# Square root of the fractional mix: GpSimd power in the copies, in place of ScalarE's activation

## The chip, the cores and the metric

One core of one Trainium2 chip runs the kernel. The metric is device time in microseconds (us) of one execution. Before the change it is 3354.84 us, the median of 2 runs (3348.12 and 3361.56 us). The engines are named as in the profile: PE is TensorE's matmuls, PEld its weight loads, DVE is VectorE, ACT is ScalarE, POOL is GpSimd, and SP is the queue that issues DMAs.

## What is computed

A batch of 32 images of 96 channels and 56x56 pixels goes through two residual layers, each behind a group normalisation. The first is a quantised expansion, depthwise convolution and projection. The second works on three groups of 32 channels: a gated 3x3 convolution, a fractional Fourier transform with a mix of its real and imaginary parts, and a Fourier mix; a 3x3 convolution over all 96 channels follows. The change is in the magnitude of the middle group.

```python
x = x + _L0_conv_ref(_gn(x), ...)
x = x + _L1_conv_ref(_gn(x), ...)

# inside layer 1
x_0, x_05, x_1 = (x[:, :C0], x[:, C0:C - C0], x[:, C - C0:])
...
Fre = _frft2d(x_05, _frft_mat(H, alpha), _frft_mat(W, alpha))
Mix = jnp.concatenate([Fre.real, Fre.imag], axis=1)
Mix = _group_conv(Mix, conv05_w[None] * Y[..., None, None], conv05_b, 0)
Fre_out = jax.lax.complex(Mix[:, :C1], Mix[:, C1:])
IFRFT = jnp.abs(_frft2d(Fre_out, _frft_mat(H, -alpha), _frft_mat(W, -alpha))) / (H * W)
...
out = jnp.concatenate([x_0, IFRFT, x_1], axis=1)
out = jax.lax.conv_general_dilated(out, conv2_w, (1, 1), [(1, 1), (1, 1)], ...)
```

## The kernel before

The kernel works image by image, with channels on partitions. Three streams of steps are laid into one another: the head of layer 0 (statistics, normalisation and the split of the input into a high and a low part), its body (expansion on TensorE, quantisation on ScalarE, depthwise convolution, projection) and layer 1 of the image before.

Two planners set the order. `arrange` merges the three streams step by step, by the work that each step declares for each engine. Then the class `Order` takes the instructions so recorded, works out who needs whom (`needs`), gives each a duration, a lag and, for DMAs, a transfer time (`model`), and lays them out engine by engine in simulated time (`pack`, called by `schedule`). `hold` writes the order down as it was found, so that each engine and each DMA queue takes its instructions in that order, one after the other. All durations in it are fixed formulas; for POOL it is 0.1 us and 2.25 ns per column with two wide inputs, 1.1 ns with one, and 0.5 us for up to 8 columns. Two VectorE or GpSimd instructions that `model` marks with `port` are not laid side by side.

The steps around the change, for each image:

- `split` (L704 to L710): VectorE normalises a quarter of the image into `v`, ScalarE rounds it to `hi` (L707), POOL subtracts to `lo` (L708), and POOL scales the image once, at the last quarter (L710). `hi` and `lo` feed the expansion on TensorE (L717), whose results ScalarE quantises (L662) and VectorE shifts as 32-bit words (L666).
- `group_stats` (L641 to L655): mean and variance; the reciprocal root is a power with exponent -0.5 on POOL over one column of 96 partitions (L654), once for each layer.
- `gate_row` and `gates`: a sigmoid (L911, L923) and a sine (L964) on ScalarE, each with a load of its table.
- `mix_f(h)` for the halves h = 0 and 1 of the image's rows: two times four matmuls (L1047) give the real and the imaginary part of four strips of 7 rows, on 4 x 32 partitions and 392 columns. ScalarE squares both into `sq` (L1054), VectorE adds them (L1055), ScalarE takes the square root in place (L1056), with a table load in front where another table was there, and POOL copies each strip to its rows of the padded image `cat` (L1060), partitions 32 to 63. `sq` is a tile of the pool `p1` with tag "Z" and one buffer, so the second half's squares need the first half's copies to be done.
- `mix_t` and `spatial` write the other two groups of `cat` from ScalarE and VectorE (L1118, L1120, L1140).
- `winograd(half, part)`: VectorE transforms `cat` (L1158, L1164, L1167); its tile `U` has the tag "Z" too. `final` is the last convolution on TensorE (L1179), and VectorE adds its results to the image (L1209 to L1220).

Of the kernel before, what the change touches and what calls it, by code (L numbers as in the profile page):

```python
# [78 lines left out]
BN_EPS = 1e-5  # L79
WINDOW, CHANGE = 3.4133, 0.09  # L80
TURNS, NEAR = 8, (2.0, 4.0, 8.0)
SLACK = 0.3


# [58 lines left out]
class Order:  # L143
# [64 lines left out]
    def model(self):  # L208


        self.took, self.lag, self.port, self.move, self.kind, self.work = [], [], [], [], [], []
        for i, e, access in zip(self.ins, self.eng, self.access):
            outs, ins = [a for a, w in access if w], [a for a, w in access if not w]
            n = max([_count(a) for a, _ in access], default=1)
            psum = [self.tiles.get(a.tensor.name, "")[:2] == "ps" for a in ins]
            wide = [a for a in ins if _count(a) > 1]
            lag = {"PE": 0.2, "Pool": 0.08}.get(e, 0.04)
            port, move, kind, work = False, 0.0, None, 0.0
            if i.opcode == "DMACopy":
                took = 0.47 if e == "SP" else 0.4  # L220
                for a in (outs[0], ins[0]):
                    run = size = _bytes(a.dtype)
                    dims, n = list(a.ap), 1.0
                    if self.tiles.get(a.tensor.name, "dram") != "dram":
                        n = dims.pop(0)[1]
                        move = max(move, _count(a) * size / 7000.0 * min(n / 16.0, 1.0))
                    for _, c in dims:
                        n *= c
                    for step, c in reversed(dims):
                        if step * size == run or c == 1:  # L230
                            run *= c
                        else:
                            break
                    run = min(run, n * size / 16)
                    move = max(move, math.ceil(n * size / run / 16) * (0.011 + run / 21e3))
                lag = 1.6 + move + (0.3 if ins[0].tensor.name.startswith(("in_x", "sd", "gd")) else 0.0)
            elif e == "PE":
                cols, weights, rows = _count(ins[0]), _count(ins[1]), ins[0].ap[0][1]
                full = all(str(a.dtype) == "dt.float32" for a in ins)
                beside = weights in (G, 64) and cols >= HN  # L240
                if i.is_transpose:
                    took = max(cols / 1175.0, 0.055)
                    work = cols / 1200.0
                elif full:
                    took = 2 * max(cols / 1175.0, min(weights * 0.85e-3, 1.0), 0.05)
                    work = cols / 600.0
                else:
                    took = max(cols / (2180.0 if "float32r" in str(ins[1].dtype) else 2350.0), 0.05)
                    work = cols / 2400.0
                if beside and not i.is_transpose:  # L250
                    took, work = took * weights / 128.0, work * weights / 128.0
                kind = (0 if rows <= 32 else 1 if rows <= 64 else 2), weights if beside else 0
                work *= rows / 128.0
            elif e == "Activation":
                out = _count(outs[0])
                bias = sum(_count(a) == 1 for a in ins) > 1
                took = 0.1 + bias * 0.1 + out / 960.0 + (0.08 if out > 700 and psum[0] else 0.13 if out < 8 else 0.0)
            elif e == "DVE":
                port = n > 8 and not any(psum)
                if port and i.opcode == "TensorScalarPtr" and len(wide) == 1:  # L260
                    took = 0.15 + n / 1920.0 + (0.12 if n >= 700 else 0.0)
                else:
                    port = port and len(wide) > 1
                    took = (0.14 if n > 8 else 0.16) + n / 960.0 + (0.06 if any(psum) and "ScalarPtr" in i.opcode else 0.0)
            elif e == "Pool":
                port = True
                took = 0.1 + n * (2.25 if len(wide) > 1 else 1.1) / 1000.0 if n > 8 else 0.5
            else:
                took = 0.1
            self.took.append(took)  # L270
            self.lag.append(lag)
            self.port.append(port)
            self.move.append(move)
            self.kind.append(kind)
            self.work.append(work)

    def pack(self, before, rank, near=0.0, back=False):

        n = len(self.ins)
        then, lacks, ready = [[] for _ in range(n)], [len(p) for p in before], [0.0] * n
        for k, p in enumerate(before):
            for q in p:
                then[q].append(k)
        engines = sorted(set(self.eng))
        free, held = dict.fromkeys(engines, 0.0), dict.fromkeys(("DVE", "Pool"), 0.0)
        soon, now = {e: [] for e in engines}, {e: [] for e in engines}
        start, end, kind, moved = [0.0] * n, [0.0] * n, None, 0.0
        window, much, fast = 0, 0.0, False  # L290
        for k in range(n):
            if not lacks[k]:
                heapq.heappush(soon[self.eng[k]], (0.0, k))
        for _ in range(n):
            t, e = min((free[e] if now[e] else max(free[e], soon[e][0][0]), e) for e in engines if now[e] or soon[e])
            while soon[e] and soon[e][0][0] <= t:
                k = heapq.heappop(soon[e])[1]
                heapq.heappush(now[e], (rank[k], k))
            k = now[e][0][1]
            if e == "PE" and near and self.kind[k] != kind:  # L300
                k = min([x for x in now[e] if self.kind[x[1]] == kind and x[0] < rank[k] + near], default=now[e][0])[1]
            if k == now[e][0][1]:
                heapq.heappop(now[e])
            else:
                now[e].remove((rank[k], k))
                heapq.heapify(now[e])
            if self.port[k]:
                t = max(t, held["Pool" if e == "DVE" else "DVE"])
            took = self.took[k]
            start[k], end[k] = t, t + took  # L310
            if e == "PE" and not back:
                took += CHANGE if kind != self.kind[k] else 0.0
                kind = self.kind[k]
                x, left = t, took
                while left > 1e-9:
                    while x >= (window + 1) * WINDOW - 1e-9:
                        window, fast, much = window + 1, much > 0.365 * WINDOW, 0.0
                    pace = 1.0 if fast else 0.5
                    part = min(left, ((window + 1) * WINDOW - x) * pace)
                    much += self.work[k] * part / took  # L320
                    left, x = left - part, x + part / pace
                end[k] = x
            free[e] = end[k]
            if self.port[k]:
                held[e] = end[k]
            lag = self.lag[k]
            if self.move[k] and not back:
                moved = max(moved, end[k] + 0.63) + self.move[k]
                lag = moved + self.lag[k] - self.move[k] - 0.63 - end[k]
            for q in then[k]:  # L330
                first = q if back else k
                alike = self.eng[q] == e and self.ins[first].opcode != "DMACopy"
                ready[q] = max(ready[q], end[k] + (0.0 if alike else self.lag[q] if back else lag))
                lacks[q] -= 1
                if not lacks[q]:
                    heapq.heappush(soon[self.eng[q]], (ready[q], q))
        return start, end
# [110 lines left out]
def block_kernel(ctx: ExitStack, tc: tile.TileContext, out: bass.AP, a: dict):  # L448
# [154 lines left out]

    mhalf = cp.tile([C, 1], F32, tag="mhalf", name="mhalf")
    nc.vector.memset(mhalf, -0.5)


    hids = []
# [245 lines left out]
    def layer1(i):  # L854
# [186 lines left out]
        def mix_f(h):  # L1041
# [11 lines left out]
                    )  # L1053
                nc.scalar.activation(sq[:, q, :], ps[:, :HN], AF.Square)  # L1054
            nc.vector.tensor_tensor(sq[:, 0, :], sq[:, 0, :], sq[:, 1, :], ALU.add)  # L1055
            nc.scalar.activation(sq[:, 0, :], sq[:, 0, :], AF.Sqrt)  # L1056
            for j in range(4):
                r = 1 + 14 * j + 7 * h
                src = sq[G * j : G * (j + 1), 0, :].rearrange("p (h w) -> p h w", w=W)
                nc.gpsimd.tensor_copy(cat[G : 2 * G, r : r + 7, 1 : 1 + W], src)  # L1060

        def transpose(g):

# [456 lines left out]
```

## Time and profile before

| What | Value |
|---|---|
| Median of 2 runs | 3354.84 us |
| Profiled execution, as a run | 3364.8 us |
| Profiled execution, span | 3363.0 us |
| Mean granted TensorE clock | 0.949 of full speed |
| ScalarE's square roots (L1056), 64 | 33.9 us busy |
| Table loads at L1056, 32 of 1283 ns | 41.1 us |
| Table loads at L911 and L964, 32 each | 41.1 us each |
| Copies to `cat` (L1060), 256 | 157.8 us busy, 616 ns mean |
| Subtractions `lo` (L708), 128 | 243.4 us |
| Image scaling (L710), 32 | 95.0 us |
| Powers with one column (L654), 64 | 36.0 us |

The span is the time from the first to the last instruction of one execution on the chip, and the rest of its run lies around it. Busy times are sums over one engine's instructions; engines work side by side, so they don't add up to the span. Idle time before an instruction is put down to the one that released it last. Matmul ends are modelled, and spans on POOL are rough.

### The profile page before, as it was taken

What the parts mean: (1) busy time and instruction counts of PE and PEld (TensorE: products, weight loads), DVE (VectorE), ACT (ScalarE), POOL (GpSimd) and SP (SyncE); (2) the same over time, 40 slices, a digit from 0 to 9 for tenths busy, and PEclk for the clock granted to TensorE, in tenths of its full rate; (3) what the DMA queues carried; (4) which work ended last, traced back from release to release, by engine and by line L of the source; (5) the groups of instructions that cost most, each with busy time, mean ns of one, the idle gap of its engine ahead of it and who ended that gap; (6) DMA issues with size and microseconds to landing.
All of it is one profiled execution on the core that took longest, in us unless ns stands there. A gap on an engine that the chain in (4) does not pass through costs nothing. (4 is left out here: it accounts for less than half of the span.)

```text
span 3363.0 us, 47042 instructions
## 1 busy us (share of the span) xinstructions
PE 2961.3 (88%) x17024; PEld 1824.1 (54%) x17024; DVE 2331.5 (69%) x4497; ACT 2085.9 (62%) x2792; POOL 585.2 (17%) x657
## 2 busy tenths in 40 slices
PE   3789998889998889999899999898998898999987
PEld 2455565455565555555455565455565455565544
DVE  5357677677777676777677777676777676777755
ACT  3566665576666566656566666566666576666543
POOL 3122101222101222111222011222111222101100
PEclk9898999999999999999999999999999999999987
DMA  4545564455655455654455655455655455655432
GB/s 125 150 118 143 147 166 133 116 144 144 167 159 141 117 145 137 168 141 134 124 146 151 173 146 149 121 146 138 168 157 142 116 145 143 166 162 148 115 89 51
DMA packets 436800, 469.92 MB, mean 140 GB/s; under 512 B 203174, under 2 KB 351640, under 8 KB 435544
## 3 DMA queue, kind: packets, MB, share of 16 engines
q1 hardware_dynamic: 432384, 464.18, 51.6%
q10 hardware_dynamic: 4184, 2.74, 0.3%
q8 instruction: 135, 2.21, 0.3%
q14 instruction: 97, 0.79, 0.1%
HBM read 266.85 MB, written 199.97 MB: 139 GB/s over the span
## 5 line engine op out<-in xcount | busy, mean ns | idle before, releaser
L662 ACT ACTIVATE q2s<-pd,o,s 128x784 uint8<-128x784 f32 x576 | 558.3, 1002 | 473.9 <-PE pd L756 454.5
L1179 PE MATMUL pc<-V,wcw 96*96 96x392 f32 x2304 | 834.9, 502 | 18.1 <-DVE V L1164 18.1
L662 ACT ACTIVATE q1s<-pe,o,s 128x784 uint8<-128x784 f32 (+1 forms) x640 | 624.1, 1004 | 219.7 <-PE pe L717 213.5
L717 PE MATMUL pe<-hi,w1r 96*128 96x392 f32 x1280 | 532.7, 416 | 68.0 <-ACT q1s L662 32.1
L1179 PEld LDWEIGHTS pc<-V,wcw 96*96 96x96 f32 x2304 | 366.9, 164 | 338.9 <-issue 319.7
L756 PE MATMUL pd<-d,dw 128*64 128x392 fp8e4 x4608 | 471.1, 345 | 85.1 <-DMA d<-sd 78.2
L717 PE MATMUL pe<-lo,w1r 96*128 96x392 f32 x1280 | 440.6, 344 | 3.2 <-POOL lo L708 3.2
L756 PEld LDWEIGHTS <-dw 128*64 128x64 bf16 x4608 | 243.3, 113 | 297.8 <-DMA d<-sd 104.8
L717 PEld LDWEIGHTS pe<-hi,w1r 96*128 96x128 f32 x1280 | 242.9, 190 | 181.4 <-ACT q1s L662 88.2
L708 POOL TENSOR_TENSOR lo<-v,hi 96x784 fp32r<-96x784 f32 x128 | 243.4, 1901 | 287.9 <-ACT hi L707 274.6
L1047 PE MATMUL pz<-F,g 98*32 98x392 f32 x1024 | 178.0, 700 | 129.3 <-DMA F<-pd 79.3
L786 PE MATMUL pp<-q,w3q 128*96 128x392 fp8e4 x1280 | 269.5, 359 | 12.1 <-DMA q<-gd 9.5
L717 PEld LDWEIGHTS pe<-lo,w1r 96*128 96x128 f32 x1280 | 244.2, 191 | 27.5 <-POOL lo L708 4.2
L786 PEld LDWEIGHTS <-w3q 128*96 128x96 fp8e4 x1280 | 167.2, 135 | 154.4 <-issue 70.6
L666 DVE TENSOR_SCALAR q2s<-q2s 128x392 uint32<-128x392 uint32 x288 | 119.4, 421 | 182.9 <-ACT q2s L662 180.0
L796 DVE SCALAR_TENSOR_TENSOR x<-pp,s,x 96x392 f32<-96x392 f32 x256 | 146.1, 617 | 103.9 <-PE pp L786 103.7
L654 POOL TENSOR_TENSOR stb<-veb,mhalf 96x1 f32<-96x1 f32 x32 | 17.9, 561 | 1143.8 <-DVE veb L653 1143.8
L1060 POOL COPY cat<-sq 32x392 f32<-32x392 f32 x256 | 157.8, 616 | 295.7 <-ACT sq L1056 286.1
L666 DVE TENSOR_SCALAR q1s<-q1s 128x436 uint32<-128x436 uint32 (+1 forms) x320 | 122.6, 389 | 120.5 <-ACT q1s L662 99.6
L704 DVE TENSOR_SCALAR v<-x,sta 96x784 f32<-96x784 f32 x128 | 87.0, 680 | 161.1 <-POOL lo L708 139.5
L1126 PE MATMUL ps<-s,g 128*128 128x392 f32 x512 | 193.6, 503 | 0.0
L1140 ACT ACTIVATE cat<-ps,b 32x392 f32<-32x392 f32 x256 | 158.8, 620 | 46.2 <-PE ps L1126 42.5
(156 smaller groups left out, 4267.8 us busy)
## 6 DMA issues: line engine op xcount, KB each, us to landing
d<-sd SPq DMA_DIRECT2D x288, 435.5 KB
gd<-q2s SPq DMA_DIRECT2D x288, 196.0 KB
sd<-q1s SPq DMA_DIRECT2D x256, 218.0 KB
q<-gd SPq DMA_DIRECT2D x128, 392.0 KB
x<-in_x_dram SPq DMA_DIRECT2D x128, 294.0 KB
out_dram<-x SPq DMA_DIRECT2D x128, 294.0 KB
pd<-pq SPq DMA_DIRECT2D x32, 808.5 KB
F<-pd SPq DMA_DIRECT2D x64, 392.0 KB
```

What stands on the lines that cost most here:

```text
L662: nc.scalar.activation(dst, ps, AF.Relu, bias=offset, scale=scale)
L666: nc.vector.tensor_scalar(w, w, 4, 0x0F0F0F0F, ALU.logical_shift_right, ALU.bitwise_and)
L708: nc.gpsimd.tensor_tensor(s["lo"][:, u, :], v, s["hi"][:, u, :].bitcast(F32), ALU.subtract)
L717: nc.tensor.matmul(ps[:, half, :HN], w1[:, 128 * b : 128 * (b + 1)], part[:, u, HN * half : HN * (half + 1)], start=(n == 0), stop=(n == 1),)
L756: nc.tensor.matmul(ps[64 * t : 64 * (t + 1), half, :HN], dw[n][:, 2 * t + y, :], view(s["d"][b, g][:, t, :], PQ * (14 * half + y), [[PQ, 1 ...
L786: nc.tensor.matmul(ps[:C, half, :HN], w3[:, b * C : (b + 1) * C], q2[b][:, u, HN * half : HN * (half + 1)], start=(b == 0), stop=(b == NB ...
L796: nc.vector.scalar_tensor_tensor(part, src, A3, part, ALU.mult, ALU.add)
L1047: nc.tensor.matmul(ps[G * j : G * (j + 1), :HN], s["g1"][: 3 * G + 2, G * q : G * (q + 1)], s["F"][:, 2 * HN * j + HN * h : 2 * HN * j + H ...
L1060: nc.gpsimd.tensor_copy(cat[G : 2 * G, r : r + 7, 1 : 1 + W], src)
L1126: nc.tensor.matmul(ps[:, :HN], s["g0"][:, 128 * t : 128 * (t + 1)], view(s0, PQ * (14 * half + t // 2) + t % 2, [[PQ, 14], [1, HH]]), star ...
L1140: nc.scalar.activation(dst, src, AF.Identity, bias=b0[2 * G : C], scale=1.0)
L1179: nc.tensor.matmul(ps[:C, :HN], wc[:, k, C * dx : C * (dx + 1)], V[:, :, dx : dx + W], start=(dx == 0), stop=(dx == 2),)
```

## The change

The square root on ScalarE is dropped. The four copies of each half become element-wise two-input instructions on GpSimd that raise the sum of squares to a power, with a constant 0.5 as the second input, and write it to the same rows of `cat`. The second input is a column of 128 partitions that is read with steps of zero over 7 x 56 elements. The planner that sets the order of all engines is changed as well: each DMA's lag is 0.2 us longer (`MARGIN`), and the time up to which the transfers have moved is kept for each issuing engine instead of one for all. The lines of `mix_f` stand 3 further down in the changed kernel.

```diff
+MARGIN = 0.2
 SLACK = 0.3
...
-                lag = 1.6 + move + (0.3 if ins[0].tensor.name.startswith(("in_x", "sd", "gd")) else 0.0)
+                lag = 1.6 + MARGIN + move + (0.3 if ins[0].tensor.name.startswith(("in_x", "sd", "gd")) else 0.0)
...
-        start, end, kind, moved = [0.0] * n, [0.0] * n, None, 0.0
+        start, end, kind, moved = [0.0] * n, [0.0] * n, None, {}
...
             if self.move[k] and not back:
-                moved = max(moved, end[k] + 0.63) + self.move[k]
-                lag = moved + self.lag[k] - self.move[k] - 0.63 - end[k]
+                moved[e] = max(moved.get(e, 0.0), end[k] + 0.63) + self.move[k]
+                lag = moved[e] + self.lag[k] - self.move[k] - 0.63 - end[k]
...
     mhalf = cp.tile([C, 1], F32, tag="mhalf", name="mhalf")
     nc.vector.memset(mhalf, -0.5)
+    half = cp.tile([128, 1], F32, tag="half", name="half")
+    nc.vector.memset(half, 0.5)
...
             nc.vector.tensor_tensor(sq[:, 0, :], sq[:, 0, :], sq[:, 1, :], ALU.add)
-            nc.scalar.activation(sq[:, 0, :], sq[:, 0, :], AF.Sqrt)
             for j in range(4):
                 r = 1 + 14 * j + 7 * h
                 src = sq[G * j : G * (j + 1), 0, :].rearrange("p (h w) -> p h w", w=W)
-                nc.gpsimd.tensor_copy(cat[G : 2 * G, r : r + 7, 1 : 1 + W], src)
+                power = view(half, 0, [[0, 7], [0, W]])[G * j : G * (j + 1)]
+                nc.gpsimd.tensor_tensor(cat[G : 2 * G, r : r + 7, 1 : 1 + W], src, power, ALU.pow)
```

## Prediction

> **What bounds the kernel now.** I read the page's engine shares first, then the line views of the instructions that the change touches, then the timeline around one of them. The sum below is made against the profiled execution: span 3363.0 us, 3364.8 us as a run, which lies 0.3% above the median of 3354.84 us.
>
> ```profile
> PE 2961.3 (88%) x17024; PEld 1824.1 (54%) x17024; DVE 2331.5 (69%) x4497; ACT 2085.9 (62%) x2792; POOL 585.2 (17%) x657
> ```
>
> TensorE is the engine with the least idle time: some 400 us in 32 images, and a period of about 105 us per image (3363 / 32). GpSimd (POOL) is idle 83% of the time. Nothing in this line says that POOL matters; whether it will depends only on what one power costs there. So the next view is that of single lines: minimum, median and maximum of one instruction in ns.
>
> ```profile
> L1056 ACT ACTIVATE sq<-sq x64: 517/531/545, 221.5 to 3325.3; 128x392 f32<-128x392 f32 x64
> L1056 ACT ACT_TABLE_LOAD  x32: 1283/1283/1283, 220.2 to 3319.7; - x32
> ...
> L1060 POOL COPY cat<-sq x256: 502/510/2198, 222.2 to 3329.3; 32x392 f32<-32x392 f32 x128
> ...
>   ACT sq L1054: 72.5, 24
>   DVE U L1158: 23.2, 31
> ...
> L992 POOL TENSOR_TENSOR cs<-ee,tab x64: 282/298/363, 172.6 to 3295.4; 114x57 f32<-114x57 f32 x64
> ...
> L708 POOL TENSOR_TENSOR lo<-v,hi x128: 1831/1846/2202, 42.6 to 3139.2; 96x784 fp32r<-96x784 f32 x128
> ...
> L654 POOL TENSOR_TENSOR stb<-veb,mhalf x32: 546/547/740, 134.4 to 3275.1; 96x1 f32<-96x1 f32 x32
> ```
>
> The first two lines are what goes: a square root of 531 ns on ScalarE, 64 times, and a table load of 1283 ns ahead of every second one. The third is what is replaced: eight copies of 392 columns per image, four for each half. The two lines under it are the waits on these copies: ScalarE's squares of the second half (72.5 us in 24 waits) and VectorE's first Winograd step (23.2 us in 31). The last three are all two-input POOL instructions; L654 is the one that matters, since it is already a power, with one column.
>
> ```profile
> 412.41 2.96 POOL L710 TENSOR_SCALAR x<-x,ab 96x3136 f32<-96x3136 f32 x1 [0.85 <-DVE v L704]
> ...
> 413.61 2.17 DVE L1055 TENSOR_TENSOR sq<-sq 128x392 f32<-128x392 f32 x1 [1.30 <-ACT sq L1054]
> 415.34 2.20 POOL L708 TENSOR_TENSOR lo<-v,hi 96x784 fp32r<-96x784 f32 x1
> ...
> 417.60 2.16 POOL L1060 COPY cat<-sq 32x392 f32<-32x392 f32 x4
> ...
> 419.79 0.50 ACT L1054 ACTIVATE sq<-pz 128x392 f32<-128x392 f32 x1 [3.44 <-POOL cat L1060]
> ```
>
> Start, length, engine. VectorE's add L1055 takes 568 ns at its median. Here it starts 1.20 us into POOL's L710 and lasts until 0.41 us after L710's end at 415.37: it was held for the rest of the other engine's instruction. So a POOL instruction that reads SBUF holds up a VectorE instruction with two SBUF inputs until it is over. The last line shows the other tie: ScalarE stands for 3.44 us, until the four copies have read `sq`, because the tile has one buffer (tag "Z").
>
> **The change part by part.**
>
> *Removed from ScalarE:* 64 x 0.531 + 32 x 1.283 = 34 + 41 = 75 us. The tables for the sigmoid and the sine are still loaded once per image each (the build of the changed kernel has 64 loads in the loop, against 96), so nothing is loaded in place of the third. These 75 us stand in the chain add, root, copies, Winograd; as a gain they are worth at most 75 us and at least nothing, as ScalarE is busy only 62%. I count them in full where the chain is what is waited for.
>
> *The copies become powers.* 256 instructions of 392 columns, in the same places of POOL's queue or interleaved with the `lo` subtractions. Their price d is in no row, so I bound it. From L992 and L708 a two-input instruction costs (1846 - 298) / (784 - 57) = 2.13 ns per column and 298 - 57 x 2.13 = 177 ns to start. The power L654 with one column takes 549 ns (547 and 551 in its two groups), so 549 - 177 - 2 = 370 ns belong to the power itself. One end: all of the 370 ns is set-up, paid once per instruction, and columns then stream as in a subtraction: d = 177 + 370 + 392 x 2.13 = 1.38 us. The other end: the 370 ns is the work on one column and repeats with each: d = 177 + 392 x 372 = 146 us. The ends lie a factor of 100 apart. The nearest row is the power itself, not the subtraction, so I take a price of L654's kind: a routine that is gone through per column, of which some is entry. No row splits the 370 ns; I take half and half: d = 177 + 185 + 392 x 187 = 73.7 us. Let f be the share that repeats; f = 0.5 here.
>
> [...]
>
> *Sum.* The powers take 256 x 73.7 = 18,867 us in the place of 158 us of copies. What hides that? POOL takes its queue in order: behind the first four powers stand, in most images, the other four, then the `rstd` power L654 of the next layer 1, and in many images `lo` subtractions that the next image's expansion needs. ScalarE's second squares wait for the first four powers (the wait above, 3.44 us for four copies of 0.51 us and what delayed them), and behind them in ScalarE's order stand the quantisations L662 that free TensorE's PSUM pairs. VectorE is held by the port, and its Winograd steps wait for the last four. So nearly nothing runs beside a power: VectorE gets one held instruction through between one power and the next. Of its instructions per image some 65 have inputs in SBUF alone (L666 19, L1158 8, L1217 6, L704, L885, L1164 and L1213 4 each, and smaller ones); 8 gaps let 8 of 65 pass, an eighth of the 105 us period, 13 us per image, 420 us in all. 3,365 + 18,867 - 158 - 75 - 420 = 21,580, so **21,600 us**.
>
> *The order by hand.* The planner is also changed: 0.2 us more for each DMA, and DMAs of different queues no longer behind one another in its model. It prices the power as any two-input instruction (0.1 + 392 x 2.25 / 1000 = 0.98 us), so it leaves no room for more. The order of every engine shifts. TensorE's waits on DMAs that could grow or go are 78 + 105 us (`d`) and 79 us (`F`): between -262 and +262 us; I take zero, as neither sign is favoured. The `half` constant is one 128x1 memset on VectorE ahead of the loops, under 0.2 us by its 1-column rows.
>
> **The rivals.** In all of them a chance is given beside the time.
>
> *The power streams (faster).* d = 1.38 us. POOL gains 256 x 1.38 - 158 = 195 us and stays under 25%; ScalarE loses 75 us. The chain of one half changes from 1.28 / 2 + 0.53 + 4 x 0.544 (the spacing of the copies) = 3.35 us to 5.5 us; TensorE has the next image's expansion to run meanwhile, and of its waits only 18 us fall on the Winograd transform, so the longer chain is covered and the shorter ScalarE shows: 3,365 - 75 = 3,290 us. If no part of 64 x (5.52 - 2.18) = 214 us is covered it is 3,365 + 214 - 75 = 3,504 us. For it: plain POOL instructions stream, and a first call can carry set-up. Against it: a copy of one column takes 183 ns (L1094, 64x1) and a subtraction starts with 177 ns, the power takes three times that, and every time, not the first time alone. It decides where L1060's successor records below about 2 us. Chance 0.16.
>
> *The power repeats, but the rest of the kernel runs beside it.* The port or the waits leave room and POOL alone is the bound: 18,867 + 585 - 158 = 19,294 us, plus 222 us ahead of the first copy and 33 us behind the last: 19,550 us. For it: some VectorE rows are not held (four L796 with a PSUM input run at 0.56 us each beside L708). Against it: ScalarE's wait and POOL's own order. Chance 0.17.
>
> *The power repeats and is exposed,* my forecast: 0.67. Inside these two, f is open: f = 1 gives 3,365 + 37,376 - 158 - 75 = 40,500 us with nothing hidden; f = 0.05 gives d = 177 + 352 + 392 x 20.6 = 8.6 us and 3,365 + 2,204 - 158 - 75 - 420 = 4,900 us. POOL alone is longer than the old run once 256 d + 427 > 3,365, from d = 11.5 us or f = 0.07.
>
> That the change does not do what it says is ruled out by the build: 256 two-input instructions with `half` stand on POOL, no square root is left in the loop.
>
> **How the numbers follow.** Repeating cases hold 0.84; with f even between 0 and 1, 0.95 of that lies above f = 0.05, so 4,900 to 40,500 us holds 0.80. Streaming, 0.16, splits into 0.10 faster by over 2% (the 3,290 us), 0.03 within 2% and 0.03 slower (part of the 214 us exposed). 2% is about what a measurement of this kernel can tell from no change. So faster 0.10, same 0.03, slower 0.84 + 0.03 = 0.87.
>
> **What would show it.** The power's own line with its median decides most: 73.7 us at f = 0.5, over 10 us for any slow case, 1.4 us for the rival. POOL busy should be near 89% of the span (19,294 of 21,600), TensorE's share fall to about 14%. `DVE sq`, `T` and `U` should wait for `cat` in hundreds of microseconds per image, ScalarE's squares for 4 d per image. If POOL is above 97%, the second rival holds. VectorE instructions that last as long as a power show the held port; if none does, that step is wrong though the sum may stand. A power line below 2 us makes the whole forecast wrong.

## The result and the profile after

The changed kernel takes 19,285.67 us (median of 2 runs, 19,280.35 and 19,291.0), 5.75 times the time before (95% interval 5.73 to 5.77). The page of its profiled execution opens with the busy time of each engine; the second fence below has answers by line: first minimum, median and maximum in ns of one instruction, then who waited for it, in us in all and number of waits.

```profile
span 19278.6 us, 46882 instructions
...
PE 3143.8 (16%) x17024; PEld 1962.7 (10%) x17024; DVE 2365.0 (12%) x4498; ACT 2011.6 (10%) x2696; POOL 16575.8 (86%) x657
...
L1063 POOL TENSOR_TENSOR cat<-sq,half 32x392 f32<-32x392 f32 x256 | 16141.9, 63054 | 136.6 <-DVE sq L1058 123.0
```

```profile
L1063 POOL TENSOR_TENSOR cat<-sq,half x256: 62827/62832/64502, 201.6 to 19182.3; 32x392 f32<-32x392 f32 x128
...
  ACT sq L1057: 7802.5, 32
  DVE U L1161: 3979.4, 32
  DVE T L1170: 3973.7, 32
...
L657 POOL TENSOR_TENSOR stb<-veb,mhalf x32: 547/548/802, 131.2 to 18693.7; 96x1 f32<-96x1 f32 x32
```

One power of 392 columns takes 62.8 us, and there are 256 of them: 16,142 us of the 19,279. The power with one column costs what it did. GpSimd goes from 17% to 86%; the other engines do about the work they did (TensorE 3144 us against 2961), and stand for the rest. The stages of one image show where. The first fence is GpSimd's timeline, one whole image; the second the busy time of each engine in the first four powers, the last four, and the stretch between images (sum line left out).

```profile
7983.88 251.53 POOL L1063 TENSOR_TENSOR cat<-sq,half 32x392 f32<-32x392 f32 x4 [0.56 <-DVE sq L1058]
8235.50 1.85 POOL L711 TENSOR_TENSOR lo<-v,hi 96x784 fp32r<-96x784 f32 x1
8237.91 253.19 POOL L1063 TENSOR_TENSOR cat<-sq,half 32x392 f32<-32x392 f32 x4 [0.57 <-DVE sq L1058]
8524.71 0.79 POOL L657 TENSOR_TENSOR stb<-veb,mhalf 96x1 f32<-96x1 f32 x1 [33.61 <-DVE veb L656]
...
8581.65 251.53 POOL L1063 TENSOR_TENSOR cat<-sq,half 32x392 f32<-32x392 f32 x4
```

```profile
core 0: us, PE busy (x) PEld busy (x) DVE busy (x) ACT busy (x) POOL busy (x), PEclk, DMA share, GB/s
7984.00:8235.00 251.00, 5.92 (x31) 3.81 (x29) 4.77 (x9) 0.00 (x0) 250.83 (x4) 0.52 0.00 0
8235.00:8491.00 256.00, 8.53 (x24) 7.08 (x24) 5.35 (x6) 8.71 (x10) 255.16 (x6) 0.50 0.02 5
8491.00:8582.00 91.00, 82.44 (x481) 49.16 (x482) 63.01 (x126) 54.01 (x74) 11.69 (x13) 0.95 0.54 146
```

In the 507 us of an image's powers TensorE works 14 us, ScalarE 9 and VectorE 10. In the 91 us between them TensorE works 82. So the image is two parts in a row, the powers and nearly all of the old 105-us period.

### The profile page after: what moved, and what is told of

It is laid out like the page before. It is cut to its first block, busy times and chain, and to the rows that moved or that the text cites. A ratio compares the mean times of both kernels' runs of the same rounds, so it can differ in the third digit from the quotient of the medians.

```text
span 19278.6 us, 46882 instructions
## 1 busy us (share of the span) xinstructions
PE 3143.8 (16%) x17024; PEld 1962.7 (10%) x17024; DVE 2365.0 (12%) x4498; ACT 2011.6 (10%) x2696; POOL 16575.8 (86%) x657
## 4 chain that ended last, share of the span: by engine, by line
POOL 77%; PE 9%; issue 8%; ACT 2%; DMA 2%; DVE 1%; POOLq 0%; SPq 0%; ACTq 0%; DVEq 0%
POOL cat L1063 76%; PE pc L1182 4%; PE pd L759 1%; PE pe L720 1%; PE pv L1016 1%; PE pi L1005 1%; PE ps L1129 1%; ACT q2s L665 1%; ACT q1s L665 0%; DMA xh<-xd 0%; DMA pd<-pq 0%; POOLq L1519 0%; POOL x L713 0%; DMA d<-sd 0%; POOL lo L711 0%
## 5 line engine op out<-in xcount | busy, mean ns | idle before, releaser
L1063 POOL TENSOR_TENSOR cat<-sq,half 32x392 f32<-32x392 f32 x256 | 16141.9, 63054 | 136.6 <-DVE sq L1058 123.0
L1182 PE MATMUL pc<-V,wcw 96*96 96x392 f32 x2304 | 880.0, 534 | 7847.3 <-DVE V L1167 7846.1
L720 PE MATMUL pe<-hi,w1r 96*128 96x392 f32 x1280 | 583.1, 456 | 6144.1 <-ACT q1s L665 3709.4
L1058 DVE TENSOR_TENSOR sq<-sq 128x392 f32<-128x392 f32 x64 | 75.2, 1176 | 7504.8 <-ACT sq L1057 4233.0
L720 PEld LDWEIGHTS pe<-hi,w1r 96*128 96x128 f32 x1280 | 290.5, 227 | 6259.5 <-ACT q1s L665 3763.9
L1057 ACT ACTIVATE sq<-pz 128x392 f32<-128x392 f32 x128 | 59.5, 495 | 7833.2 <-POOL cat L1063 7802.5
L1170 DVE TENSOR_TENSOR T<-cat 96x1624 f32<-96x1624 f32 x64 | 118.1, 1846 | 3974.8 <-POOL cat L1063 3973.7
L1161 DVE SCALAR_TENSOR_TENSOR U<-cat 96x812 f32<-96x812 f32 x64 | 63.8, 997 | 3979.4 <-POOL cat L1063 3979.4
L720 PE MATMUL pe<-lo,w1r 96*128 96x392 f32 x1280 | 510.8, 399 | 182.4 <-POOL lo L711 182.4
L720 PEld LDWEIGHTS pe<-lo,w1r 96*128 96x128 f32 x1280 | 296.9, 232 | 196.9 <-POOL lo L711 184.0
```

Of the source, the lines that this page charges most:

```text
L720: nc.tensor.matmul(ps[:, half, :HN], w1[:, 128 * b : 128 * (b + 1)], part[:, u, HN * half : HN * (half + 1)], start=(n == 0), stop=(n == 1),)
L1063: nc.gpsimd.tensor_tensor(cat[G : 2 * G, r : r + 7, 1 : 1 + W], src, power, ALU.pow)
L1170: nc.vector.tensor_tensor(by_row, d4(2), d4(0), ALU.subtract)
L1182: nc.tensor.matmul(ps[:C, :HN], wc[:, k, C * dx : C * (dx + 1)], V[:, :, dx : dx + W], start=(dx == 0), stop=(dx == 2),)
```

## The experiments

**The planner's edits alone, and the powers replaced by multiplications.** The change touches the order of all engines besides the power, so the two were parted.

```diff
 # e1_planner: the kernel before, and of the change only
+MARGIN = 0.2
...
+                lag = 1.6 + MARGIN + move + ...
...
+                moved[e] = max(moved.get(e, 0.0), end[k] + 0.63) + self.move[k]
```

> The kernel before with the planner's two edits alone (0.2 us more lag for each DMA, transfers kept apart by queue); the root stays on ScalarE and the copies stay copies. Theory (the powers are the whole loss): within 1% of before, 3320 to 3390 us, as waits on DMAs are only some 260 us in all and can shift either way. Rival (the new order of the engines carries part of the loss): slower than before by more than 2%, over 3420 us.

```diff
 # e2_mult: the changed kernel, and
-                nc.gpsimd.tensor_tensor(cat[...], src, power, ALU.pow)
+                nc.gpsimd.tensor_tensor(cat[...], src, power, ALU.mult)
```

> The changed kernel with a multiplication by the constant 0.5 in the place of the power: the same instructions, operands and places, but the root is left out of the computation. It shows what the change would be worth if a power streamed like other two-input instructions. Theory: one instruction takes 177 + 392 x 2.13 ns = 1.01 us, and the time falls to about 3290 us, by the 75 us taken off ScalarE. Rival: ScalarE's 75 us are worth nothing since TensorE is the bound, and the time is that of the planner's edits alone, 3320 to 3390 us.

The planner's edits alone give 3322.49 us, 0.9906 of before (0.9879 to 0.9932): the theory holds, and the planner's edits by themselves cost nothing. With the multiplication the time is 3405.82 us, 1.0145 of before (1.0108 to 1.0181). In the traces every engine and the DMA queue take the same instructions in the same order as in the changed kernel, so the power's own price is the whole of the other 15,880 us. GpSimd's group line (busy us, mean ns), and minimum, median and maximum of one instruction:

```profile
L1063 POOL TENSOR_TENSOR cat<-sq,half 32x392 f32<-32x392 f32 x256 | 267.9, 1046 | 162.7 <-DVE sq L1058 149.4
...
L1063 POOL TENSOR_TENSOR cat<-sq,half x256: 830/834/2875, 198.6 to 3375.9; 32x392 f32<-32x392 f32 x128
```

The mean of 1046 ns is near the streaming price that was worked out (1.01 us), but by chance: most take 834 ns, and some that last longer, up to 2875 ns, raise the mean. The time is not as expected: neither 3290 us nor the 3320 to 3390 us of the rival. That is taken up below.

**What a power's price goes by.**

```diff
 # e3_widths: the changed kernel, and
+                m = (7, 4, 2, 1)[j]
-                nc.gpsimd.tensor_tensor(cat[... r : r + 7 ...], src, power, ALU.pow)
+                nc.gpsimd.tensor_tensor(cat[... r : r + m ...], src[:, :m], power[:, :m], ALU.pow)
+                if m < 7:
+                    nc.gpsimd.tensor_copy(cat[... r + m : r + 7 ...], src[:, m:])
```

> The changed kernel with powers of 7, 4, 2 and 1 rows of 56 in the four strips of a half (392, 224, 112, 56 columns) and plain copies of the other rows, whose root is left out. Theory (price per column, straight from 548 ns at one column to 62,832 ns at 392, 159.3 ns per column): 36.1, 18.2 and 9.3 us for 224, 112 and 56 columns, and a run of 3365 + 64 x 126.4 - 75 - 158 = 11,200 us. Rival (a fixed cost per instruction beyond the first column, or one per row of the pattern): the shorter ones lie above that line, at 20 us or more for 56 columns.

```diff
 # e4_wide: the changed kernel, and
+            nc.gpsimd.tensor_tensor(sq[:, 0, :], sq[:, 0, :], view(half, 0, [[0, HN]]), ALU.pow)
             for j in range(4):
...
-                nc.gpsimd.tensor_tensor(cat[...], src, power, ALU.pow)
+                nc.scalar.copy(cat[...], src)
```

> The power is taken once per half in place on all 128 partitions and 392 columns; ScalarE makes the four copies to the padded image. Theory (price by columns, all partitions side by side): one power takes 62.8 us, 64 of them 4020 us, and the run is 3365 + 4020 - 75 to 158 less plus up to 123 us of ScalarE's copies, 7150 to 7350 us. Rival (price by elements): one power takes 4 x 62.8 = 251 us, and the run stays near 19,300 us.

GpSimd's groups of the widths run, kept apart by shape, and under them that of the wide one:

```profile
L1064 POOL TENSOR_TENSOR cat<-sq,half 32x392 f32<-32x392 f32 x64 | 4022.8, 62856 | 124.2 <-DVE sq L1058 122.0
L1064 POOL TENSOR_TENSOR cat<-sq,half 32x224 f32<-32x224 f32 x64 | 2305.0, 36015 | 3.7
L1064 POOL TENSOR_TENSOR cat<-sq,half 32x112 f32<-32x112 f32 x64 | 1175.3, 18365 | 0.0
L1064 POOL TENSOR_TENSOR cat<-sq,half 32x56 f32<-32x56 f32 x64 | 592.1, 9251 | 3.8
```

```profile
L1059 POOL TENSOR_TENSOR sq<-sq,half 128x392 f32<-128x392 f32 x64 | 4026.7, 62917 | 244.5 <-DVE sq L1058 244.5
```

The four widths lie on the line through one column and 392: 9.3, 18.2 and 36.1 us were expected, 9.25, 18.37 and 36.02 measured. From 56 to 392 columns it is (62,856 - 9,251) / 336 = 159.5 ns per column, whether the pattern has one row of 56 or seven. And 128 partitions cost 62.9 us where 32 cost 62.8: the price goes by columns, and four strips of 32 partitions one after the other pay it four times. So the theories hold for the price of one power in both runs. The times, of one run each, came out higher than expected: 11,417.54 us (11,200 expected) and 7427.55 us (7150 to 7350 expected, 78 us over). The wide form does the whole computation with a quarter of the powers' time, and is still 2.2 times the kernel before.

**Why the other work does not run beside the powers.** Two causes were possible: queues laid out for a power of 0.98 us, or ties that no layout undoes. The first run tells the planners the price, the second takes away one of the two longest waits in the profile, ScalarE's for the one buffer of `sq`. The new tiles of the second run take over the tags `g0` and `h`, and the order of the engines shifts with them.

```diff
 # e5_planned: the changed kernel, and
                 took = 0.1 + n * (2.25 if len(wide) > 1 else 1.1) / 1000.0 if n > 8 else 0.5
+                if outs and outs[0].tensor.name.startswith("cat") and len(wide) > 1:
+                    port, took = False, 62.8
...
-  S(lambda h=h: mix_f(h), ... dve=0.6, pool=2.0)
+  S(lambda h=h: mix_f(h), ... dve=0.6, pool=251.0)
```

> The changed kernel with the planner told the price: a power is laid out as 62.8 us of GpSimd in both planners and without a claim on VectorE's port. The computation is the same. Theory (the powers are exposed since the queues were laid out for 0.98 us, so the engines stand at instructions that need the powers): the other work now runs beside them, GpSimd is the bound and the time falls to 256 x 62.83 + 427 + some 250 at the two ends = 16,760 us, at most 17,300. Rival (data and single buffers force the order, whatever the plan): over 18,800 us, near the 19,286 of the changed kernel. It also shows VectorE's instructions with two SBUF inputs far inside a power: if the power holds the port, they last up to 62 us; if it lets go after its start, they keep their medians.

```diff
 # e6_buffers: the changed kernel, and
-            nc.vector.tensor_tensor(sq[:, 0, :], sq[:, 0, :], sq[:, 1, :], ALU.add)
+            sm = p1.tile([128, HN], F32, tag=("g0", "h")[h], name=f"sm{i}_{h}")
+            nc.vector.tensor_tensor(sm, sq[:, 0, :], sq[:, 1, :], ALU.add)
...
-                src = sq[G * j : G * (j + 1), 0, :]...
+                src = sm[G * j : G * (j + 1)]...
```

> The changed kernel with the sum of squares in a tile apart for each half, so that ScalarE's squares and VectorE's add of the second half need not wait for the first half's powers. The planner still reckons 0.98 us. Theory (the wait on the one buffer is only one of several ties, TensorE and VectorE still stand at the Winograd steps that need all powers): within 1.5% of 19,286 us, 19,000 to 19,300. Rival (that wait is what exposes the first four powers): some 64 x 50 us of other work gets in beside them, 17,500 us or less.

They give 18,986.29 us (5.667 of before, 5.637 to 5.697) and 19,114.92 us (one run). My theory of the first fell: 16,760 us were expected. For the second it held: 0.9% less than the changed kernel. The windows of `e5_planned` show what a better layout reached and what it did not (first four powers of an image begin at 8418, the last four at 8083 for the image before):

```profile
8083.00:8336.00 253.00, 0.69 (x1) 0.29 (x1) 5.41 (x9) 0.44 (x1) 252.63 (x4) 0.50 0.00 0
8336.00:8418.00 82.00, 69.56 (x315) 41.70 (x319) 57.31 (x96) 35.63 (x54) 13.92 (x13) 0.83 0.36 90
8418.00:8671.00 253.00, 38.59 (x220) 23.70 (x212) 15.69 (x35) 27.32 (x30) 251.79 (x5) 0.58 0.09 29
```

Now 39 us of TensorE's work lie beside the first four powers, and yet the stretch without powers is 82 us, only 9 less than in the changed kernel. In the chain of waits through it stand the last convolution of one image (22 us of `pc`), the statistics of the next, its transposes, transforms, `ps`, `cat` and `pz`, and then its first power: layer 1, one step after another. Beside the last four powers TensorE does next to nothing, and the waits name the cause (us in all, number, longest):

```profile
PE pe L722 <- POOL lo L713: 7855.4, 35, 255.0
ACT sq L1059 <- POOL cat L1065: 6759.0, 32, 252.2
DVE v L709 <- POOL sta L659: 5543.5, 29, 195.2
```

The expansion needs `lo`, and on GpSimd's queue `lo` stands behind four powers. Beside the first four powers TensorE's work ends after 55 us for a like reason: VectorE's normalisation `v` needs `sta`, a power with one column, and this too stands behind four long ones. So by these waits two ties remain in this plan: GpSimd's own order, and layer 1, which contains the powers and follows itself from image to image. No run took either away. The times of the runs with powers fit: the table shows what is left per image when the powers' busy time is taken off.

| Run | Time us | Powers busy us | Rest per image us |
|---|---|---|---|
| before | 3354.84 | 0 | 104.8 |
| changed | 19,285.67 | 16,141.9 | 98.2 |
| e3_widths | 11,417.54 | 8095.2 | 103.8 |
| e4_wide | 7427.55 | 4026.7 | 106.3 |
| e5_planned | 18,986.29 | 16,139.7 | 89.0 |
| e6_buffers | 19,114.92 | 16,152.2 | 92.6 |

In every version the powers are very nearly added in full. A layout that puts `lo` and `sta` ahead of the powers, or tiles of their own for `cat` and the Winograd transform (which takes over the tags of `F` and `torus`), was not tried.

**What a cheap power would have been worth.** The multiplication run was slower than the planner's edits alone though it takes 75 us off ScalarE. Three runs part the instructions from the order that the planner finds for them, and one doubles GpSimd's share.

```diff
 # e7_copy: the changed kernel, and
-                nc.gpsimd.tensor_tensor(cat[...], src, power, ALU.pow)
+                nc.gpsimd.tensor_copy(cat[...], src)
 # e11_copy_old: the kernel before, and
-            nc.scalar.activation(sq[:, 0, :], sq[:, 0, :], AF.Sqrt)
 # e10_square: e1_planner, and
-            nc.scalar.activation(sq[:, 0, :], sq[:, 0, :], AF.Sqrt)
+            nc.scalar.activation(sq[:, 0, :], sq[:, 0, :], AF.Square)
 # e9_double: e2_mult, with each multiplication given twice
```

> The changed kernel with plain copies in the place of the powers: the root is left out of the computation, the planner's edits stay. Beside the planner's edits alone it has 64 square roots and 32 table loads less on ScalarE (75 us) and nothing else. Theory (layer 1's chain from image to image, with TensorE's work laid around it, sets the time): the root's 0.53 us and up to 1.28 us of table per image leave the chain, 17 to 58 us, 3265 to 3305 us. Rival (TensorE alone is the bound): the same as the planner's edits alone, 3322 us, within 0.4%.

> The kernel before with the root left out of the computation and nothing else: the same instructions as e7_copy, but laid out by the planner as it was. Theory (e7_copy's 3425 us come from the order that the planner happened to find): this one lies elsewhere, 3280 to 3390 us, by at least 1% from e7_copy. Rival (without the root the kernel is slower in any order): within 1% of 3425 us.

> The planner's edits alone, with a second square in the place of the square root on ScalarE (the root is left out of the computation). The planner prices both alike, so every engine has the very order of e1_planner, and only the 32 table loads of 1283 ns go. It shows what ScalarE's relief is worth with the order held fast. Theory (the loads stand in the chain from image to image, or are hidden): between 0 and 41 us less than 3322 us, 3281 to 3322 us. Rival (something in the instructions left out slowed e7_copy by 3%, not the order): over 3380 us here too.

> The multiplication run with each of its 256 instructions given twice (same operands, same place), the root left out: four more instructions of 1.05 us per half on GpSimd. Theory (chain): the second half's four stand between the add and the Winograd transform, 4.2 us for each image, 134 us in all, and up to 268 us if the first half's count too: 3540 to 3670 us against 3406 us. Rival (GpSimd is idle for 79% and TensorE is the bound): within 1% of 3406 us.

| Run | Median us | Against before (95%) |
|---|---|---|
| e1_planner | 3322.49 | 0.9906 (0.9879 to 0.9932) |
| e2_mult | 3405.82 | 1.0145 (1.0108 to 1.0181) |
| e7_copy | 3424.68 | 1.0213 (1.0164 to 1.0261) |
| e11_copy_old | 3272.58 | 0.9773 (0.9745 to 0.9802) |
| e10_square | 3288.54 | 0.9824 (0.9774 to 0.9874) |
| e9_double | 3586.69 | 1.0685 (1.0645 to 1.0726) |

Both expectations of `e7_copy` failed. `e11_copy_old` has the same instructions but for one `memset` and takes 4.3% less (0.9773 / 1.0213 = 0.957): the difference between the two is the planner's edits alone, and so the order of the engines. That it would lie at least 1% from `e7_copy` held; at 3272.58 us it lies 7 us below the range given for it. TensorE's waits for two DMAs show a part of it, above in `e7_copy`, below in `e11_copy_old`:

```profile
PE pz L1050 <- DMA F<-pd: 132.0, 30, 6.8
```

```profile
PE pz L1047 <- DMA F<-pd: 64.1, 19, 5.9
```

With the order held fast (`e10_square` has that of `e1_planner`), the 32 table loads are worth 3322 - 3289 = 34 us by the medians, 0.8% by the ratios, of their 41 us; the two intervals just miss each other. So the loads are worth something, most likely near their full size, and an order found afresh can give or take more than that. Doubling the multiplications costs 3587 - 3406 = 181 us, 5.7 us per image, between the 4.2 us of one half's four and the 8.4 us of both: this fits the theory that GpSimd's work between the add and the Winograd transform counts, though GpSimd is idle for three quarters of the time. But the order is laid out afresh here too, and two orders lay 152 us apart above, so how much of the 181 us is GpSimd's work is not shown.

**A version without the power that computes the whole.** ScalarE takes the root strip by strip into the padded image, with the planner's edits and without them.

```diff
 # e8_direct: e1_planner, and e12_direct_old: the kernel before, and
-            nc.scalar.activation(sq[:, 0, :], sq[:, 0, :], AF.Sqrt)
...
-                nc.gpsimd.tensor_copy(cat[...], src)
+                nc.scalar.activation(cat[...], src, AF.Sqrt)
```

> The planner's edits alone, but ScalarE takes the root strip by strip straight into the padded image: 256 square roots of 32x392 in the place of 64 of 128x392, and no copies on GpSimd. The computation is the same. Theory (chain): one root of 0.53 us and four copies of 0.544 us become four roots of about 0.5 us, 0.7 us less per half, about 22 to 45 us less than 3322 us. Rival (ScalarE's time counts): its 256 x 0.5 - 34 = 94 us more delay the quantisations that free TensorE's banks, and it is slower than 3322 us by up to 94 us.

> The kernel before with ScalarE's root taken strip by strip straight into the padded image, as in e8_direct, but laid out by the planner as it was. The computation is the same. Theory (the order that the planner finds is worth more than the edit): 3280 to 3400 us, and at least 0.7% from e8_direct's 3314 us. Rival (the edit itself carries e8_direct's gain): within 0.5% of 3314 us.

3313.58 us, 0.9867 of before (0.9831 to 0.9904), and 3339.67 us, 0.9965 (0.9934 to 0.9997). The first is faster than the kernel before and the changed one, and has the lowest median of the versions that compute the whole, 1.3% under before; from the planner's edits alone (0.9906) its interval does not part it. The theory of `e12_direct_old` holds: the planner's edits are worth 1.0% here (0.9867 against 0.9965), the edit itself some 0.4% under either planner.

## Why the prediction was right

- *The power's price decides, and it repeats per column.* Right. Of the 370 ns that one column costs over a plain instruction, (159.3 - 2.1) / 370 = 0.42 repeat, where half was taken: 62.8 us in the place of 73.7 us. That the price repeats was argued from L654; that it repeats by near a half was luck, since no row spoke for one share over another, and the range from 4,900 to 40,500 us says so.
- *The sum.* With the measured busy time in the place of 18,867 us it reads 3365 + 16,142 - 158 - 75 = 19,274 us with nothing hidden; 19,286 was measured. So two terms were mis-sized: d, 2725 us too high in all, and the 420 us for VectorE instructions let through between powers, of which nothing is left in the net: some 14 us of TensorE's work per image did run beside the powers, but what is left per image is 98 us, as if nothing were hidden. The 21,600 us were 12% too high, and within the range.
- *What keeps the other work away.* Of the ties named, three are in the profile: ScalarE's squares behind the first four powers (7802 us in 32 waits), the Winograd steps behind the last four (3979 and 3974 us), and GpSimd's own order (seen in `e5_planned`'s waits for `lo` and `sta`). The fourth, VectorE held by the port for the whole of a power, is wrong; the next section shows it. The sum did not rest on it alone and stands.
- *TensorE's share near 14%, GpSimd's near 89%.* 16% and 86%.
- *The rival with GpSimd as the bound* gave 19,550 us, near the measured time by chance: with the measured price it is 16,142 + 427 + 255 = 16,824 us, and GpSimd would be above 97%.
- *The rival of a streaming power* fell with d. Its own sum was tried too: with multiplications, 834 ns at their median, the kernel takes 3406 us, not 3290, inside the span from 3290 to 3504 us that was given for it. Before and `e11_copy_old` differ by 2.3%, 77 us, near the 75 us of ScalarE, but the orders of these two differ as well. What the rival's sum left out is open: the longer chain that it took as covered, or the order, since `e7_copy` has the short chain and the planner's edits and takes 3425 us.
- *The planner's order, taken as zero between -262 and +262 us:* -32 us alone (0.9906), but up to 152 us between two orders of the same instructions (`e7_copy`, `e11_copy_old`). Within the bounds, and larger than it was weighed beside effects of 75 us.

## What to carry to other kernels

An operation is priced from a row of that very operation, not of its neighbours: a one-column power at three times the price of a one-column copy was the warning, and a second width, one run, turns it into a price per column. A price by columns means that such an operation belongs on all 128 partitions at once, not on strips (`e4_wide`: 64 powers in the place of 256). And where a planner lays out the order, hold the order fast before reading an effect below 5% as that of the edit.

## What the runs showed of the hardware that was not expected

A power does not hold the port to SBUF that GpSimd shares with VectorE for its length. L710 did so before the change; a power lets go early. In `e5_planned` four powers run from 8417.89 to 8669.41, and VectorE's 32-bit shifts, which take 365 and 387 ns at their medians, run beside them unstretched (columns: start, length, engine):

```profile
8417.89 251.52 POOL L1065 TENSOR_TENSOR cat<-sq,half 32x392 f32<-32x392 f32 x4 [25.24 <-DVE sta L650]
```

```profile
8422.03 0.36 DVE L671 TENSOR_SCALAR q2s<-q2s 128x392 uint32<-128x392 uint32 x1 [3.29 <-ACT q2s L667]
8424.94 0.39 DVE L671 TENSOR_SCALAR q1s<-q1s 128x436 uint32<-128x436 uint32 x1 [2.54 <-ACT q1s L667]
8427.71 0.39 DVE L671 TENSOR_SCALAR q1s<-q1s 128x436 uint32<-128x436 uint32 x1 [2.39 <-ACT q1s L667]
```

Instructions with two SBUF inputs pass too. In the same run three steps `V` of the Winograd transform, which read `T` twice, follow within two powers that run from 554.79 to 682.18:

```profile
554.79 127.39 POOL L1065 TENSOR_TENSOR cat<-sq,half 32x392 f32<-32x392 f32 x2
```

```profile
556.63 2.51 DVE L1163 SCALAR_TENSOR_TENSOR V<-T 96x812 f32<-96x812 f32 x3
```

That only the start is held can be read from the changed kernel. VectorE's `T` takes 1.85 us, starts just ahead of the third power of the last four, and that power lasts 64.5 us in the place of 62.83; the shift behind `T` takes 1.02 us in the place of 0.39, and no VectorE instruction lasts over 4 us in the whole run:

```profile
8363.67 1.85 DVE L1170 TENSOR_TENSOR T<-cat 96x1624 f32<-96x1624 f32 x1 [124.66 <-POOL cat L1063]
8365.43 1.02 DVE L669 TENSOR_SCALAR q1s<-q1s 128x436 uint32<-128x436 uint32 x1
```

The Trainium skill's page "SBUF — State Buffer" says in its section "SBUF: two separate sides" that the pair is an exclusive lock which the first to start keeps for the whole instruction, the other being blocked. L710 and L708 agree with it before the change (L1055 held to 0.41 us behind L710's end, and the L708 next to it at 2.20 us against 1.85 at the median); the power does not, by these rows, and the measurement decides. What in the power's code lets the port go was not tried.

The granted TensorE clock was low where TensorE stood: 0.50 to 0.52 in the windows of the changed kernel's powers, 0.95 between them, and 0.574 as a mean of the run, where the kernel before had 0.949.
